# A Mamba layer's scans: the carried state as a column of dt·u·B, dt·u·B issued mid-group, dt·u in four, and weight products beside the scans

## The chip, the cores and the metric

The kernel runs on one core of a Trainium2 chip, all in float32 except for a small part of the graph layer. The metric is the device time of one execution in microseconds, as the median of several runs. TensorE (PE) multiplies matrices, VectorE (DVE), ScalarE (ACT) and GpSimd (POOL) work on tiles of 128 partitions, and SyncE (SP) issues most transfers.

## The reference

The network has four layers on an input of 2 images, 256 channels, 48 x 48 positions (L = 2304 positions in each image). Only layer 0, the start of layer 1 and the start of layer 2 matter here.

Layer 0 is a Mamba layer with a forward and a backward branch. Each branch works on 512 inner channels with 16 states each:

```
xs = silu(causal_conv4(xi) + conv_b)
dt = softplus(proj_dt(xs) @ dtproj.T + dtproj_b)          # one value per channel and position
h[t] = exp(dt[t] * A) * h[t-1] + (dt[t] * u[t]) * B[t]     # u = xs, 16 states per channel
y[t] = sum over states of h[t] * C[t]  +  D * xs[t]
out  = x + ((y_f + y_b) * silu(z)) @ out_proj.T
```

Layer 1 begins with a group norm of each image (32 groups of 8 channels). Layer 2 begins with an attention of three heads. For each head h the kernel multiplies the weights first: the 256 x 256 products of the query's and key's weights, and of the value's and output's weights, are stacked in one array "gm", and the biases give a small array "ub".

## The kernel before

**Tiling.** Layer 0 goes through the positions in pieces of W = 384 (NCH = 6 pieces an image). For each image the forward branch runs over its six pieces, and then the backward branch over the same pieces from the last to the first: 24 pieces in the order (image 0 forward, image 0 backward, image 1 forward, image 1 backward). The 512 channels are DB = 4 blocks of 128 partitions.

**One piece.** `scan` goes through 16 groups. A group is one block d and GN = 4 of the 16 states, and blocks go in pairs (d0, d0+1). For each pair and set of states, SP loads B and C rows broadcast to all partitions (tiles bb and cc, 768 KB each). For each group POOL computes `db` = dtu * B for four states in one instruction (L359). For each state ACT computes `hs` = exp(dt*A) into PSUM (L376), DVE runs the recurrence with tensor_tensor_scan (L382 forward, L385 backward) and multiplies by C (`hc`, L390); for six of sixteen states POOL does that product instead, and then the scan writes to the tile `ho`. PE adds the 16 products of a block into PSUM by a multiplication with the identity (`yp`, L344). The scan starts from the last piece's state:

```
init = 0.0 if step == 0 else state[:, d, n : n + 1]
nc.vector.tensor_tensor_scan(to, hs, db[:, j], init, ALU.mult, ALU.add)
...
nc.scalar.copy(state[:, d, n : n + 1], last)
```

**Beside the scans.** Three generators are advanced between the states, at 32 slots a piece (one after every second state): `prepare` makes the next piece's xs, dt and dtu (15 steps, ended at slot 25), `project_in` makes the inner channels of a later piece (12 steps, over 32 slots, in the first ten pieces only), and `project_out` ends a backward piece. A pair such as `(prepare(...), 15, 25)` says how many steps there are and by which slot they are to be done. The end of `prepare` is the softplus: exponential and +1 on ACT (L302, L305), Ln and -1 on ACT (L307, L308), three 1536-wide operations on DVE (L310 to L312), and the product dtu = dt * xs on POOL in one 1536-wide instruction (L314). While scans run, `prepare`, `project_in` and `project_out` get their PSUM bank from one pool with a single bank, tag "mm".

**Order.** The code is written in this order; a scheduler of the framework then orders the instructions of each engine by priority, which is the order of the program, among those that it holds to be ready, so that small moves happen. Each engine then runs its list in order, and so does SP's queue of transfers.

**Layers 1 and 2.** Layer 1 starts with `group_norm(0)`: statistics of 12 pieces (L517), two small products with the matrix `gmat`, and the scaling into `xn` (L533). The first product of layer 1 that needs it is `pk` (L547). Beside layer 1 the edge lists of the graph layer are sorted on DVE, which `sort_rest` ends. `layer2_attn` then loads the weights of each head (`w_eo`), multiplies them (L713, L721) and copies them to `gm` and `ub`; the transposes of the values (L741) and the query product `pq` (L750, emptied by ACT into `qq`, L754) follow.

Of the kernel before, what the change touches and what calls it, by code (L numbers as in the profile page):

```python
# [27 lines left out]
P = 128  # L28
# [24 lines left out]
class Env:  # L53
# [20 lines left out]

    def uid(self):
        self.n_pools += 1
        return self.n_pools
# [7 lines left out]
def bc(ap, shape, axis):  # L85

    return ap.unsqueeze(axis).to_broadcast(shape)
# [31 lines left out]

def load_x(E, b, c):  # L120
    xin = E.p["x"].rearrange("b (k p) n -> p b k n", p=P)
    E.nc.sync.dma_start(
        E.xres[:, :, b * L + c * W : b * L + (c + 1) * W], xin[:, b, :, c * W : (c + 1) * W]
    )
# [4 lines left out]
def layer0(ctx, E):  # L129

# [32 lines left out]
    def hold():  # L163

        pool, tag = (ps, "mm") if scanning else (psh, "hs")
        return pool.tile([P, W], F32, tag=tag, name="mm")

    def project_in(b, c):
# [15 lines left out]
        rs = up.tile([P, W], F32, tag="rs", name="rs")  # L184
# [53 lines left out]
    one = big.tile([P, 2], F32, name="one")  # L238
    nc.vector.memset(one[:, 0:1], 1.0)
    nc.vector.memset(one[:, 1:2], -1.0)  # L240
# [11 lines left out]
    def prepare(b, s, c, got):  # L252
# [39 lines left out]
        dt = wp.tile([P, DB, W], F32, tag="dt", name="dt")  # L292
# [12 lines left out]
        nc.scalar.activation(dtu, ex, AF.Identity, bias=one[:, 0:1])  # L305
        yield
        nc.scalar.activation(ln, dtu, AF.Ln)  # L307
        nc.scalar.activation(dtu, dtu, AF.Identity, bias=one[:, 1:2])  # L308
        yield
        nc.vector.tensor_tensor(ex, ex, dtu, ALU.subtract)  # L310
        nc.vector.tensor_tensor(dt, dt, ln, ALU.add)
        nc.vector.tensor_tensor(dt, dt, ex, ALU.add)  # L312
        yield
        nc.gpsimd.tensor_tensor(dtu, dt, xs, ALU.mult)  # L314
        got.extend((b, s, c, xs, y, dt, dtu, bcd))
        yield

# [13 lines left out]
    def scan(step, beside, b, s, c, xs, y, dt, dtu, bcd):  # L331

        fwd = s == "f"
        yp = [None] * DB
# [17 lines left out]
        for d0, g in [(d0, g) for d0 in range(0, DB, 2) for g in range(NS // GN)]:  # L352
            bb = wp.tile([P, GN, W], F32, tag="bb", name="bb")
            nc.sync.dma_start(bb, bcd[16 + g * GN : 16 + (g + 1) * GN, :].partition_broadcast(P))
            cc = wp.tile([P, GN, W], F32, tag="cc", name="cc")
            nc.sync.dma_start(cc, bcd[32 + g * GN : 32 + (g + 1) * GN, :].partition_broadcast(P))
            for d in (d0, d0 + 1):
                db = wp.tile([P, GN, W], F32, tag="db", name="db")
                nc.gpsimd.tensor_tensor(db, bc(dtu[:, d, :], [P, GN, W], 1), bb, ALU.mult)  # L359
                if g == 0:  # L360

                    while waiting and waiting[0][1] < d0:
                        add_state(*waiting.pop(0)[1:])
                    yp[d] = psy.tile([P, W], F32, tag=f"y{d % 2}", name=f"yp{d}")
                    nc.tensor.matmul(
                        yp[d], lhsT=w_d[s][:, d, :], rhs=xs[:, d, :], start=True, stop=False
                    )
                    if not fwd:
                        nc.tensor.matmul(
                            yp[d], lhsT=E.ident, rhs=yf[:, d, :], start=False, stop=False  # L370
                        )
                for j in range(GN):
                    n = g * GN + j
                    on_pool = j in GP[(g + d) % 2]
                    hs = psh.tile([P, W], F32, tag="hs", name="hs")
                    nc.scalar.activation(  # L376
                        hs, dt[:, d, :], AF.Exp, scale=nega[s][:, d * NS + n : d * NS + n + 1]
                    )
                    to = wp.tile([P, W], F32, tag="ho", name="ho", bufs=4) if on_pool else hs
                    init = 0.0 if step == 0 else state[:, d, n : n + 1]  # L380
                    if fwd:
                        nc.vector.tensor_tensor_scan(to, hs, db[:, j], init, ALU.mult, ALU.add)  # L382
                        last = to[:, W - 1 : W]
                    else:
                        nc.vector.tensor_tensor_scan(  # L385
                            to[:, ::-1], hs[:, ::-1], db[:, j, ::-1], init, ALU.mult, ALU.add
                        )
                        last = to[:, 0:1]
                    hc = wp.tile([P, W], F32, tag="hcp" if on_pool else "hc", name="hc", bufs=4)
                    (nc.gpsimd if on_pool else nc.vector).tensor_tensor(hc, to, cc[:, j, :], ALU.mult)  # L390
                    if step < NCH - 1:
                        nc.scalar.copy(state[:, d, n : n + 1], last)  # L392
                    while waiting and waiting[0][0] + LAG <= at:
                        add_state(*waiting.pop(0)[1:])
                    if on_pool:
                        waiting.append((at, d, hc))
                    else:
                        add_state(d, hc)
                    at += 1
                    if j % 2:  # L400
                        slot += 1
                        for i, (steps, n_steps, end) in enumerate(beside):
                            while done[i] * end < n_steps * slot and next(steps, beside) is not beside:
                                done[i] += 1
# [4 lines left out]
        for steps, _, _ in beside:  # L409
            for _ in steps:  # L410
                pass

# [7 lines left out]
    for _ in prepare(0, "f", 0, ready):  # L420
        pass
    scanning = True
    pieces = [(0, c) for c in range(2, NCH)] + [(1, c) for c in range(NCH)]
    after = None
    for i, (b, s, step, c) in enumerate(order):
        now, ready = ready, []
        beside = [(after, 2, 5)] if after else []
        if i + 1 < len(order):
            nb, s2, _, c2 = order[i + 1]
            beside.append((prepare(nb, s2, c2, ready), 15, 25))  # L430
        if i < len(pieces):
            beside.append((project_in(*pieces[i]), 12, 32))
        scan(step, beside, *now)
# [26 lines left out]
def layer1(ctx, E, edges):  # L460
# [21 lines left out]
    gmat = big.tile([P, P], F32, name="gmat")  # L482
    same_block(E, lw, gmat, 3, 1.0 / 8)
# [26 lines left out]
    def group_norm(b):  # L510

        xb = E.xres[:, :, b * L : (b + 1) * L]
        mv = wp.tile([P, 2, 2], F32, tag="mv", name="mv")
        for k in range(2):
            st = wp.tile([P, NCH, 6], F32, tag="st", name="st")
            for c in range(NCH):
                nc.vector.bn_stats(st[:, c, :], xb[:, k, c * W : (c + 1) * W])  # L517
            nc.vector.bn_aggr(mv[:, k, :], st)
        pg = ps.tile([P, 2], F32, tag="mm", name="pg")
        nc.tensor.matmul(pg, lhsT=gmat, rhs=mv[:, :, 0], start=True, stop=True)  # L520
        gm = wp.tile([P, 2], F32, tag="gm", name="gm")
        nc.vector.tensor_copy(gm, pg)
        dv = wp.tile([P, 2], F32, tag="dv", name="dv")
        nc.vector.tensor_tensor(dv, mv[:, :, 0], gm, ALU.subtract)
        nc.vector.tensor_tensor(dv, dv, dv, ALU.mult)
        nc.vector.tensor_tensor(dv, dv, mv[:, :, 1], ALU.add)
        gv = ps.tile([P, 2], F32, tag="mm", name="gv")
        nc.tensor.matmul(gv, lhsT=gmat, rhs=dv, start=True, stop=True)
        gr = wp.tile([P, 2], F32, tag="gr", name="gr")
        nc.scalar.activation(gr, gv, AF.Sqrt, bias=E.eps[1e-5])  # L530
        nc.vector.reciprocal(gr, gr)
        for k in range(2):
            nc.vector.tensor_scalar(  # L533
                E.xn[:, k, b * L : (b + 1) * L], xb[:, k, :], gm[:, k : k + 1], gr[:, k : k + 1],
                ALU.subtract, ALU.mult,
            )
# [150 lines left out]
def layer2_attn(ctx, E):  # L687
# [3 lines left out]

    nc, tc, p = E.nc, E.tc, E.p
    NH, D = 3, 768
    S = L // NH
    DT, ST, HW2 = D // P, S // P, S // 2
# [4 lines left out]
    ub = big.tile([P, NH, 4], F32, name="ub")  # L700
    with (
        tc.tile_pool(name="l2wt", bufs=2) as wts,
        tc.tile_pool(name="l2wps", bufs=2, space=PSUM) as ps,
    ):
        for h in range(NH):

            w_eo = wts.tile([P, DT, 2 * C], F32, tag="w_eo", name="w_eo")
            nc.sync.dma_start(w_eo[:, :, 0:C], p["W_embed"][h].rearrange("(k p) m -> p k m", p=P))
            nc.sync.dma_start(w_eo[:, :, C:], p["W_outT"].rearrange("(k p) m -> p k m", p=P))
            for m in range(2):  # L710
                pg = ps.tile([P, 2 * C], F32, tag="pg", name="pg")
                for k in range(DT):
                    nc.tensor.matmul(  # L713
                        pg, lhsT=w_eo[:, k, m * P : (m + 1) * P], rhs=w_eo[:, k, :],
                        start=k == 0, stop=k == DT - 1,
                    )
                nc.vector.tensor_copy(gm[:, h, m, :], pg)
# [1248 lines left out]
```

## Time and profile before

| | us |
|---|---|
| median of 3 runs | 5448.44 (5447.45 to 5450.56) |
| the profiled execution | 5416.49 |
| its span, from the first to the last instruction | 5414.7 |
| first db product (L359) of the scans | 95.9 |
| last output product of layer 0 starts | 2398 |
| first pk of layer 1 (L547) | 2417.2 |
| first pq of layer 2 (L750) | 3181.6 |

A row of the profile names an operation by the engine, the line of the kernel and the tile that it writes and reads ("hs<-hs,state,db"). Times are microseconds unless marked ns. A fence with starts is a timeline: start, duration, engine, line, operation. A fence with "<-" between two operations is a list of waits: who waited, for whom, and then the total in us, how many times, and the longest. The row of busy tenths has 40 slices of 135 us each.

### The profile page before, as it was taken

The page shows a single profiled execution, that of the slowest core. Times are in us where ns is not written, and L with a number is a line of the kernel's source. Part 1 is how long each engine was busy: PE and PEld are TensorE (multiplying, and loading weights), DVE is VectorE, ACT ScalarE, POOL GpSimd, SP SyncE. Part 2 cuts the span into 40 slices and gives each one's busy share as a digit, 9 for nine tenths or more (in the row PEclk, how much of TensorE's full clock was granted, in tenths as well). Part 3 has the DMA queues.
Part 4 walks back from the last instruction along what each step waited for, and adds up shares of the span by engine and source line. Part 5 has one row for each costly group of instructions (what it writes and reads, how often), then busy time and mean ns, then how long its engine had stood idle before and what let it go on. Part 6 is the DMA issues. An engine that isn't in the chain of part 4 may idle for free. (4 is left out here: it accounts for less than half of the span.)

```text
span 5414.7 us, 47212 instructions
## 1 busy us (share of the span) xinstructions
PE 4771.7 (88%) x15246; PEld 2653.7 (49%) x15246; DVE 3503.3 (65%) x5360; ACT 2365.8 (44%) x4935; POOL 2410.2 (45%) x1308
## 2 busy tenths in 40 slices
PE   7888888888877778769999999999999999999897
PEld 3444444443333334335555555556654455555675
DVE  4899898898999898899996234447634401212343
ACT  5767777666667666632222213332123222222111
POOL 3888887788999888860000000008802100000321
PEclk8999999999999889989999989999999999999898
DMA  4445454443545444431110010011122200000422
GB/s 162 163 170 179 161 177 171 156 150 140 172 148 178 152 152 158 146 138 33 40 38 6 0 39 0 27 36 30 22 71 55 61 3 9 6 9 8 84 82 93
DMA packets 178083, 491.28 MB, mean 91 GB/s; under 512 B 32182, under 2 KB 100666, under 8 KB 177562
## 3 DMA queue, kind: packets, MB, share of 16 engines
q1 hardware_dynamic: 169114, 475.36, 25.6%
q0 software_dynamic: 8704, 12.73, 1.6%
q8 instruction: 124, 2.03, 0.2%
q14 instruction: 141, 1.16, 0.1%
HBM read 416.44 MB, written 71.58 MB: 90 GB/s over the span
## 5 line engine op out<-in xcount | busy, mean ns | idle before, releaser
L344 PE MATMUL yp<-hc,ident 128*128 128x384 f32 x3072 | 1203.1, 525 | 291.6 <-DVE hc L390 251.7
L359 POOL TENSOR_TENSOR db<-dtu,bb 128x1536 f32<-128x1536 f32 x384 | 1332.3, 3471 | 49.7 <-issue 19.1
L344 PEld LDWEIGHTS yp<-hc,ident 128*128 128x128 f32 x3072 | 577.1, 199 | 873.5 <-DVE hc L390 447.6
L390 POOL TENSOR_TENSOR hc<-ho,cc 128x384 f32<-128x384 f32 x576 | 579.4, 1014 | 185.3 <-DVE ho L382 83.3
L390 DVE TENSOR_TENSOR hc<-hs,cc 128x384 f32<-128x384 f32 x960 | 498.5, 540 | 39.1 <-PE yp L344 37.8
L376 ACT ACTIVATE hs<-dt,negab 128x384 f32<-128x384 f32 x768 | 434.2, 581 | 93.3 <-DVE ho L385 42.1
L376 ACT ACTIVATE hs<-dt,negaf 128x384 f32<-128x384 f32 x768 | 433.4, 581 | 55.0 <-DVE hc L390 25.5
L385 DVE TENSOR_TENSOR_SCAN hs<-hs,state,db 128x384 f32<-128x384 f32 x400 | 395.1, 1010 | 56.0 <-POOL db L359 30.3
L382 DVE TENSOR_TENSOR_SCAN hs<-hs,state,db 128x384 f32<-128x384 f32 x400 | 396.1, 1010 | 30.2 <-POOL db L359 22.9
L1771 POOL DMA_INDIRECT xe<-xt_d,token x48 | 47.4, 987 | 754.3 <-issue 716.0
L266 PE MATMUL mm<-xw,w_cv 128*128 128x384 f32 x768 | 287.5, 510 | 67.2 <-ACT xs L270 29.4
L1706 PE MATMUL po<-at,xtok 128*128 128x384 f32 x864 | 329.9, 507 | 7.7 <-ACT at L1704 7.5
L912 POOL PARTITION_ALL_REDUCE most<-most x1 | 0.4, 380 | 738.6 <-DVE most L911 738.6
L1697 PE MATMUL sp<-qT,xn 128*128 128x384 f32 x864 | 317.4, 487 | 0.0
L1704 ACT ACTIVATE at<-sp 128x384 f32<-128x384 f32 x216 | 104.6, 490 | 472.7 <-PE sp L1697 472.6
L1354 PE MATMUL ph<-xn,w 128*128 128x384 f32 x768 | 288.2, 519 | 19.3 <-ACT hid L1358 7.6
L627 PE MATMUL pf<-t,wfc 128*128 128x384 f32 x768 | 255.5, 489 | 0.0
L646 PE MATMUL po<-hid,wfc 128*128 128x384 f32 x768 | 253.6, 486 | 0.0
L385 DVE TENSOR_TENSOR_SCAN ho<-hs,state,db 128x384 f32<-128x384 f32 x240 | 240.0, 1000 | 15.2 <-ACT hs L376 15.1
L382 DVE TENSOR_TENSOR_SCAN ho<-hs,state,db 128x384 f32<-128x384 f32 x240 | 239.5, 998 | 8.4 <-ACT hs L376 8.2
L266 PEld LDWEIGHTS mm<-xw,w_cv 128*128 128x128 f32 x768 | 145.9, 196 | 195.1 <-ACT xs L270 46.9
L392 ACT COPY state<-hs 128x1 f32<-128x1 f32 x800 | 117.5, 155 | 278.2 <-DVE hc L390 276.3
(433 smaller groups left out, 7947.6 us busy)
## 6 DMA issues: line engine op xcount, KB each, us to landing
bb<-bcd SPq DMA_DIRECT2D x192, 768.0 KB, 4.1
cc<-bcd SPq DMA_DIRECT2D x192, 768.0 KB, 4.1
xw<-xi_d SPq DMA_DIRECT2D x24, 774.0 KB, 5.3
w<-in_m_w SPq DMA_DIRECT2D x16, 1024.0 KB, 5.8
y_d<-y SPq DMA_DIRECT2D x32, 384.0 KB, 2.3
ye<-y_d SPq DMA_DIRECT2D x32, 384.0 KB, 3.5
xi_d<-xz SPq DMA_DIRECT2D x48, 192.0 KB, 3.0
z_d<-xz SPq DMA_DIRECT2D x48, 192.0 KB, 3.2
```

The source lines that it names most:

```text
L266: nc.tensor.matmul(px, lhsT=w_cv[b, s][:, d * 4 + k, :], rhs=xw[:, d, o : o + W], start=k == 0, stop=k == 3,)
L344: nc.tensor.matmul(yp[d], lhsT=E.ident, rhs=hc, start=False, stop=summed[d] == NS)
L359: nc.gpsimd.tensor_tensor(db, bc(dtu[:, d, :], [P, GN, W], 1), bb, ALU.mult)
L376: nc.scalar.activation(hs, dt[:, d, :], AF.Exp, scale=nega[s][:, d * NS + n : d * NS + n + 1])
L382: nc.vector.tensor_tensor_scan(to, hs, db[:, j], init, ALU.mult, ALU.add)
L385: nc.vector.tensor_tensor_scan(to[:, ::-1], hs[:, ::-1], db[:, j, ::-1], init, ALU.mult, ALU.add)
L390: (nc.gpsimd if on_pool else nc.vector).tensor_tensor(hc, to, cc[:, j, :], ALU.mult)
L627: nc.tensor.matmul(pf, lhsT=wfc1[:, k, f * P : (f + 1) * P], rhs=t1[:, k, :], start=k == 0, stop=k == 1,)
L646: nc.tensor.matmul(po[m], lhsT=wfc2[:, f, m * P : (m + 1) * P], rhs=hid[:, i, :], start=f == 0, stop=f == 15,)
L1354: nc.tensor.matmul(ph, lhsT=w1[:, e, k, f * P : (f + 1) * P], rhs=xn[:, k, c * W : (c + 1) * W], start=k == 0, stop=k == 1,)
L1697: nc.tensor.matmul(sp, lhsT=xn[:, k, t0 + i * P : t0 + (i + 1) * P], rhs=qT[:, k, c * W : (c + 1) * W], start=k == 0, stop=k == 1,)
L1706: nc.tensor.matmul(po[m], lhsT=xtok[:, i, m * P : (m + 1) * P], rhs=at, start=i == 0, stop=i == MT - 1,)
```

## The change

Five things are done:

1. **State as a column.** The tiles hs, ho, db and dt (now `dts`) get one column more, ahead of the piece in the scan's direction. dts is 0 there, so that exp gives 1; db holds the last piece's state there, which POOL copies from `state` (a memset of 0 in a first piece). The scan starts from the immediate 0.0, over 385 columns, and its first result is the carried state.
2. **db mid-group.** `begin_group` issues the loads of bb and cc and the db of the next group (at a piece's end the next piece's first) after the second state of the current one.
3. **Softplus and dtu.** L308 goes; its -1 is done in a scalar_tensor_tensor on DVE. The three DVE operations have a step each, with an empty step after Ln, and dtu is four 384-wide instructions in four steps. `prepare` has 21 steps now, to be done by slot 29.
4. **Weight products.** `head_products` computes gm and ub in twelve parts beside pieces 10 to 21, one part of three steps a piece, and stores gm to DRAM (`gm_d`). Layer 2 loads it back.
5. **Group statistics.** `group_stats` of image 0 run beside the second forward piece of image 1; layer 1 only scales. `gmat` is built at the start of the kernel. In layer 3 one normalization takes its buffers from a pool of its own with single buffers.

The core of the diff:

```diff
-    def scan(step, beside, b, s, c, xs, y, dt, dtu, bcd):
+    def begin_group(q, first_piece, b, s, c, xs, y, dts, dtu, bcd):
+        d0, g, d = groups[q]
+        if d == d0:
+            for n, o in (("bb", 16), ("cc", 32)):
+                held[n] = wp.tile([P, GN, W], F32, tag=n, name=n)
+                nc.sync.dma_start(held[n], bcd[o + g * GN : o + (g + 1) * GN, :].partition_broadcast(P))
+        lead, body = (0, slice(1, W + 1)) if s == "f" else (W, slice(0, W))
+        db = wp.tile([P, GN, W + 1], F32, tag="db", name="db")
+        nc.gpsimd.tensor_tensor(db[:, :, body], bc(dtu[:, d, :], [P, GN, W], 1), held["bb"], ALU.mult)
+        if first_piece:
+            nc.gpsimd.memset(db[:, :, lead : lead + 1], 0.0)
+        else:
+            nc.gpsimd.tensor_copy(db[:, :, lead], state[:, d, g * GN : (g + 1) * GN])
+        return db, held["cc"]
...
-                    hs = psh.tile([P, W], F32, tag="hs", name="hs")
+                hs = psh.tile([P, 512], F32, tag="hs", name="hs")[:, : W + 1]
...
-                        nc.vector.tensor_tensor_scan(to, hs, db[:, j], init, ALU.mult, ALU.add)
+                nc.vector.tensor_tensor_scan(
+                    to[:, way], hs[:, way], db[:, j, way], 0.0, ALU.mult, ALU.add
+                )
...
+                if j == 1:
+                    if q + 1 < len(groups):
+                        begun = begin_group(q + 1, step == 0, b, s, c, xs, y, dts, dtu, bcd)
+                    elif following:
+                        begun = begin_group(0, step == NCH - 1, *following)
```

In `prepare`:

```diff
+        dts = wp.tile([P, DB, W + 1], F32, tag="dt", name="dt")
+        nc.vector.memset(dts[:, :, lead : lead + 1], 0.0)
+        dt = dts[:, :, body]
...
         nc.scalar.activation(ln, dtu, AF.Ln)
-        nc.scalar.activation(dtu, dtu, AF.Identity, bias=one[:, 1:2])
         yield
-        nc.vector.tensor_tensor(ex, ex, dtu, ALU.subtract)
+        yield
+        nc.vector.scalar_tensor_tensor(ex, dtu, -1.0, ex, ALU.add, ALU.subtract)
+        yield
         nc.vector.tensor_tensor(dt, dt, ln, ALU.add)
-        nc.vector.tensor_tensor(dt, dt, ex, ALU.add)
         yield
-        nc.gpsimd.tensor_tensor(dtu, dt, xs, ALU.mult)
+        nc.vector.tensor_tensor(dt, dt, ex, ALU.subtract)
+        yield
+        for d in range(DB):
+            nc.gpsimd.tensor_tensor(dtu[:, d, :], dt[:, d, :], xs[:, d, :], ALU.mult)
+            yield
...
-            beside.append((prepare(nb, s2, c2, ready), 15, 25))
+            beside.append((prepare(nb, s2, c2, ready), 21, 29))
...
+        elif i < len(pieces) + 12:
+            beside.append((islice(heads, 3), 3, 32))
+        if (b, s, step) == (1, "f", 1):
+            beside.append((group_stats(E, up, lambda: hold()[:, 0:2], 0), 15, 32))
```

The weight products, one part for each head h, half m and half z of the inner dimension:

```diff
+                t = up.tile([P, 2, W], F32, tag=("pos", "h", "sq")[k], name="w_eo")
+                t = t.rearrange("p k w -> p (k w)")[:, : 2 * C]
+                nc.sync.dma_start(t[:, 0:C], p["W_embed"][h, rows, :])
+                nc.sync.dma_start(t[:, C:], p["W_outT"][rows, :])
...
+            pg = ps.tile([P, 2 * C], F32, tag="mm", name="pg")
+            for k in range(3):
+                nc.tensor.matmul(pg, lhsT=w_eo[k][:, m * P : (m + 1) * P], rhs=w_eo[k], start=k == 0, stop=k == 2)
+            if z == 0:
+                nc.scalar.copy(part, pg)
+            else:
+                nc.vector.tensor_tensor(part, part, pg, ALU.add)
+                nc.sync.dma_start(E.gm_d[h, m], part)
+            yield
+            pu = ps.tile([P, 2 * C], F32, tag="mm", name="pu")
...
```

In layer 2 the loop over the heads with its loads and products goes, and this takes its place:

```diff
+    for h in range(NH):
+        nc.sync.dma_start(gm[:, h], E.gm_d[h].rearrange("m p c -> p m c"))
```

`group_stats(E, wp, bank, b)` holds the statistics part of the old `group_norm` unchanged, with a yield after each bn_stats and each small step, 15 steps in all.

## The prediction

> **What bounds the kernel now.** I read the page's busy table and slices first, then equal-length windows over single scan pieces, then the waits of VectorE and GpSimd inside the scan stage, then the timeline at the places which the diff touches.
>
> ```profile
> PE 4771.7 (88%) x15246; PEld 2653.7 (49%) x15246; DVE 3503.3 (65%) x5360; ACT 2365.8 (44%) x4935; POOL 2410.2 (45%) x1308
> DVE  4899898898999898899996234447634401212343
> POOL 3888887788999888860000000008802100000321
> ```
>
> The shares of the whole span mislead: VectorE (DVE) is at 65%, but in slices 2 to 17, the 96 to 2392 us of the scans, it is at 8 or 9 tenths with GpSimd (POOL) close behind. Afterwards TensorE (PE) is at 9 and POOL is idle. So the diff touches two regimes. The starts of the dtu product (L314) lie one piece apart; windows between them cut out a forward piece of batch 1, a forward and a backward piece of batch 0 (both with a projection beside them) and a backward piece of batch 1:
>
> ```profile
> 1527.20:1616.60 89.40, 71.53 (x193) 33.55 (x192) 86.67 (x108) 61.94 (x155) 82.56 (x41) 0.98 0.45 159
> 358.60:455.10 96.50, 79.59 (x225) 39.55 (x224) 89.51 (x114) 69.46 (x168) 83.14 (x43) 1.00 0.49 169
> 854.30:958.60 104.30, 87.99 (x250) 44.89 (x249) 91.32 (x119) 72.31 (x166) 81.30 (x42) 0.98 0.46 163
> 2094.20:2190.40 96.20, 75.39 (x208) 38.37 (x208) 85.41 (x114) 64.70 (x153) 81.29 (x41) 0.96 0.44 156
> ```
>
> The columns are PE, weight loads, DVE, ACT, POOL. DVE idles 2.7, 7.0, 13.0 and 10.8 us of a piece: the plain forward piece is DVE-bound, the others lose time to waits. Over the stage these are the largest:
>
> ```profile
> DVE hs L382 <- POOL db L359: 39.1, 34, 6.8
> DVE hc L390 <- PE yp L344: 37.8, 33, 9.7
> DVE hs L385 <- POOL db L359: 35.3, 34, 2.5
> DVE dt L311 <- ACT state L392: 24.4, 12, 3.6
> DVE ho L385 <- ACT hs L376: 18.7, 14, 2.9
> ```
>
> They come at one place of each piece, about 70% through, where Ln, its table loads, three wide DVE steps (L310 to L312) and the wide dtu product follow each other. Outside the scans one line matters: between layers 1 and 2, ACT's first qq waits 58.7 us for PE, which multiplies weights by weights.
>
> ```profile
> ACT qq L754 <- PE pq L750: 96.6, 23, 58.7
> ```
>
> **The scan's initial value: -74 us of DVE.** With an operand, two scans hold DVE for 1.83 us until the next start (0.915 each); with the immediate 0.0 of a first piece, for 1.71 (0.855 each):
>
> ```profile
> 359.95 1.02 DVE L382 TENSOR_TENSOR_SCAN hs<-hs,state,db 128x384 f32<-128x384 f32 x1
> 360.87 1.00 DVE L382 TENSOR_TENSOR_SCAN ho<-hs,state,db 128x384 f32<-128x384 f32 x1
> 361.78 0.54 DVE L390 TENSOR_TENSOR hc<-hs,cc 128x384 f32<-128x384 f32 x1
> ...
> 120.85 0.95 DVE L382 TENSOR_TENSOR_SCAN hs<-hs,db 128x384 f32<-128x384 f32 x1
> 121.72 0.93 DVE L382 TENSOR_TENSOR_SCAN ho<-hs,db 128x384 f32<-128x384 f32 x1
> 122.56 0.53 DVE L390 TENSOR_TENSOR hc<-hs,cc 128x384 f32<-128x384 f32 x1
> ```
>
> The page has 400+240+400+240 = 1280 scans with an operand: 1280 x 0.06 = 77 us. The 385th column costs about 0.855/384 = 2 ns on all 1536, 3 us. That is 3.7 us less DVE work in each of 20 pieces. The memset of dts' zero column (four elements, some 0.07 us like the memsets at the start) counts nothing on DVE: 24 x 0.07 = 2 us at worst.
>
> **The state column: POOL gets 384 small copies or memsets.** None is in the trace. From below I take 0.10 us (POOL's 128x1 memsets). From the two POOL products, 1014 ns for 384 elements and 3439 for 1536, the slope is 2.1 ns and the intercept 0.21 us; I take that, with 0.10 and the 1.0 us of a whole 384-wide product as ends. 16 x 0.21 = 3.4 us a piece. Behind each copy in POOL's queue stand that group's products hc, and the scans wait for the copy. Its source was written by ACT one piece earlier, so it waits for nothing itself.
>
> **Softplus and dtu.** ACT loses L308, 24 x 1.57 = 38 us, and the DVE steps move one scheduling slot (3 us) apart, with an empty slot after Ln. The DVE waits of L311 (24.4 on ACT's state copy, 7.5 on Ln) and L310 (4.4 and 1.3) should end: -38. The waits of the scans for ACT's exponentials, 18.7+13.1+11.2+9.3+10.7 = 63, fall by half, because the table loads remain: -31. The dtu product is 3.43 us in one block; in four (4 x 0.955) other POOL work passes between, and with db issued mid-group I take half of the 74 us of waits for db away: -37. The new slots 21 of 29 end dtu by slot 29; db of the next piece starts at 31, so 2 slots of cover remain; without it a piece boundary would show up to 4 us of waiting.
>
> Against this speaks a lock, and here row and rule differ:
>
> ```profile
> 1609.91 4.95 POOL L359 TENSOR_TENSOR db<-dtu,bb 128x1536 f32<-128x1536 f32 x1
> 1611.96 4.51 DVE L312 TENSOR_TENSOR dt<-dt,ex 128x1536 f32<-128x1536 f32 x1
> ```
>
> Alone these take 3.44 and 1.74; overlapping, both stretch. Yet the median of L312 is 1.742, and all three steps together average (44.0+45.0+53.6)/23 = 6.2 us a piece against 3 x 1.74 = 5.2, since today POOL mostly stands idle in that burst. The rows alone would add nothing for the new order. The Trainium skill, "SBUF — State Buffer", "Who interferes with whom", says that a DVE instruction with two SBUF inputs and a GpSimd instruction that reads SBUF exclude each other for the whole instruction. If so, spreading the steps into a busy POOL makes each collide: the mean rest of a POOL instruction is (16 x 3.4² + 28 x 0.955²)/(2 x 81) = 1.3 us, so 3 x 1.3 = 3.9 a piece instead of 1.0: +67 us over 23 pieces for DVE, and POOL is held 3 x 1.74 = 5.2 us a piece. I take the rule, since the plain forward piece (L310 3.06, L311 1.91, L312 4.51 in one piece) already behaves so. The row would give 60 us more gain.
>
> **The scan stage summed by kind of piece.** POOL after: 16 x 3.39 + 28 x 0.955 = 81, +3.4 copies, +5.2 held = 89.5. DVE busy after: the four windows less 3.7, plus 2.9 of lock where it isn't paid today: 83.0, 88.7, 90.5, 84.6. Idle left, about half: 2.7, 2.5, 7, 6.
> - Six forward pieces of batch 1: DVE 86, POOL 89.5, as today: 0.
> - Forward, batch 0: 91.2 instead of 96.5; 5 x 5.3 and 3 for the first piece: -29.
> - Backward, batch 0: 97.5 instead of 104.3 in four of them, about 5 in the other two, which are shorter: -37.
> - Backward, batch 1: 90.6 instead of 96.2; 5 x 5.6, and 2 for the last piece, which prepares nothing: -30.
> - The prelude (dtu in four before the first db): -3.
> Sum -99, of 2296 us.
>
> **Weight products moved beside the scans.** Twelve pieces get 6 matmul records of 0.593 and 12 of about 0.2 each: 6 us of PE, which idles 18 to 21 us of these pieces; on top ACT or DVE empties a bank (0.6 or 0.7 us). They share the one "mm" bank with prepare and project_out, so PE can stand behind an emptying, and a late yp makes hc late (the 37.8 us above). Six loads of 128 KB a piece go through SP ahead of bb and cc, 6 x 0.4 = 2.4 us of issue, at 45% DMA use; the products come ten slots later, so they don't wait. I charge 0.7 us a piece, +8; ends 0 and 12 x 6 = 72.
>
> **Group statistics of batch 0.** 12 bn_stats at 0.46 and small steps, 7 us of DVE in one piece: +7. At layer 1's start this clears the path from 2399.2 to the first pk at 2417.2. Left there: the xn scaling (2.85 us, which I expect behind the 4.27 us memset of img on POOL) and wqkv's load, issued at 2398.85, some 5 us. First pk near 2406: -11, ends 0 and -15.
>
> **Layer 2's start.** PE's last layer-1 matmul ends near 3112; the first pq comes at 3181.6:
>
> ```profile
> 3118.11 5.19 PEld L721 LDWEIGHTS pu<-vec,w_eo 128*128 128x128 f32 x24 [3.14 <-issue]
> 3181.60 0.88 PE L750 MATMUL pq<-xn,gm 128*128 128x384 f32 x1
> ```
>
> After: three loads of gm (512 KB; w_eo's halves of 768 KB landed in 5.0 to 11.0), and the transposes, whose copies queue on DVE behind some 10 us of sort_rest. First pq at about 3127: -54, ends -40 and -62. The attention is PE-bound after that, so the lead stays. The matrix of the group norm is now built at the start, where DVE idles until 7.8 us and POOL until 92 (uncovered: some 1.5 us). The normalization with single buffers in layer 3 runs beside PE-bound attention (uncovered: a few us of its DVE steps once). Both 0.
>
> **Sum.** -99 +8 +7 -11 -54 = -149 on the profiled execution, 5416.5 us (span 5414.7 and 1.8 around it). The timed median is 5448.4, 0.6% more; the difference carries over as it is: about 5299.
>
> **Rivals.**
> 1. POOL becomes the bound everywhere: copies of 0.4 us, each of the steps blocking a db. Then POOL's 81 + 6.4 + 5.2 = 93, with 2 to 3 of hand-over, is today's mean piece (95.6), and the 99 us fall to nothing: -50, 5398. For it: POOL is already over 80 busy in every window. Against: it still idles 7 to 23 us there.
> 2. The lock is avoided as in today's median, and the waits end wholly: 67 + 30 us more, 5202. For it: emptying the burst is what the spread does. Against: POOL's own floor.
> 3. Slower: the small POOL copy costs far more than its elements. Pieces equal today's mean plus what layers 1 and 2 save, (95.6 + 50/24) = 97.7, when (97.7 - 0.5 - 86.1)/16 = 0.69 us a copy. At 1.0 us a piece is 86.1 + 16 + 0.5 = 102.6, +168 in the scans and -50 elsewhere: 5566. Against: even POOL's 128x128 iota takes 0.24.
> 4. Layer 2 does not start earlier, because its transposes and gm loads still queue (behind sort_rest until 3143): -20 instead of -54, 5333.
>
> **How the numbers follow.** Main case and its variant 4: 0.68, with 5255 to 5360 from the ends of its terms. Rival 1: 0.17. Rival 2: 0.09. Rival 3: 0.06. A measurement of this kernel can tell about 0.2%, 11 us, from no change. Faster 0.92, same 0.02 (rival 1 with a bad start of layer 2), slower 0.06. The range 5235 to 5405 holds the main case and most of rival 1, and leaves out rivals 2 and 3 and the far ends.
>
> **What would show it.** Right: scans 0.855 apart in all pieces; POOL copies near 0.2; L311's and L310's waits gone, these steps over 2.5 us on average; forward pieces of batch 1 at about 89, backward ones near 91 and 98; first pq 10 to 18 us after layer 1's last matmul. Wrong: POOL copies above 0.5; DVE waiting more for db than 74 us; pieces of 12 longer by PE's full 6 us; or qq still waiting 40 us or more.

## The result, and the profile after

The changed kernel takes 5440.71 us (median of 20 runs, 5430.69 to 5449.36); the kernel before, beside it on the same chip, takes 5456.51 (5447.26 to 5463.13). The ratio is 0.9972 [0.9965, 0.9978]: faster by 15 us, where 149 were forecast. The profiled execution of the changed kernel has a span of 5429.9 us.

The first traces of before and after can't be set side by side over the whole span: the products fp of layer 3, which no edit touches, last 191 us in the trace of before and 230 in that of after. As the last section shows, this goes with the chip. So both kernels were profiled once more on one chip (pair_before, pair_after). There fp lasts 229 us in both. The rows give shortest, median and longest duration in ns, then the first and the last start:

```profile
L1086 PE MATMUL fp<-wide,ol x256: 466/466/531, 3760.5 to 3989.6; 128*128 128x360 f32 x128
```

```profile
L1160 PE MATMUL fp<-wide,ol x256: 466/466/531, 3756.8 to 3985.0; 128*128 128x360 f32 x128
```

On that chip the spans, 5442.4 and 5435.0, divide like this:

| us | before | after | difference | forecast |
|---|---|---|---|---|
| start to layer 0's last output product | 2395.2 | 2451.9 | +56.7 | -84 |
| from there to the first pk | 19.0 | 6.6 | -12.4 | -11 |
| layer 1's products, pk to the last po | 691.9 | 692.6 | +0.7 | 0 |
| last po to the first pq of layer 2 | 67.4 | 14.0 | -53.4 | -54 |
| the rest | 2268.9 | 2269.9 | +1.0 | 0 |

The forecast of the first row is its -99 for the scans with +8 and +7 for the work laid beside them. Everything outside the scan stage came as written. In the first two traces the stage lost 46 us; either way the error is some 130 to 140 us, all of it in the scans. The whole scan stage of pair_before and of pair_after (the columns are the stretch and its length, then the busy time of PE, weight loads, DVE, ACT and POOL, the granted clock of PE, and the DMA's busy share and GB/s):

```profile
96.00:2395.00 2299.00, 1859.51 (x5011) 918.78 (x5012) 2083.63 (x2692) 1553.52 (x3577) 1966.52 (x986) 0.95 0.45 160
```

```profile
94.00:2452.00 2358.00, 1936.01 (x5244) 980.10 (x5242) 2067.29 (x2761) 1533.07 (x3563) 2046.91 (x1437) 0.94 0.46 160
```

DVE is busy for 16 us less (2067.3 for 2083.6), but it idles for 290.7 us instead of 215.4. The granted clock hardly differs, and a product yp lasts 526 ns on average, where it lasted 524: PE is not slower at the products that DVE waits for.

The page of the changed kernel, busy times and the tenths of DVE and POOL:

```profile
PE 4782.7 (88%) x15246; PEld 2664.3 (49%) x15246; DVE 3467.9 (64%) x5395; ACT 2340.8 (43%) x4914; POOL 2490.2 (46%) x1764
...
DVE  4988888888888888899997244546544501212343
...
POOL 3888887888898898890000000038502200000331
```

In slices 3 to 17 DVE has gone from eights and nines to eights, and POOL stands at 8, with a few sevens and nines, as before. Over the span DVE has 35 us less to do (3467.9 for 3503.3) and POOL 80 more (2490.2 for 2410.2). (POOL's digits from slice 24 on are work of later layers, with PE at 9.) The windows over one piece of each kind, between starts of the dtu product, in the order of the prediction:

```profile
1543.40:1635.40 92.00, 75.99 (x209) 38.36 (x208) 80.88 (x111) 60.39 (x156) 84.89 (x61) 0.94 0.47 167
349.10:447.40 98.30, 81.62 (x225) 41.56 (x224) 86.19 (x114) 68.92 (x168) 84.72 (x60) 0.97 0.48 165
857.60:961.90 104.30, 89.49 (x249) 46.96 (x248) 89.78 (x120) 70.85 (x166) 86.49 (x61) 0.95 0.47 164
2130.10:2228.50 98.40, 80.69 (x229) 41.06 (x228) 86.33 (x119) 64.12 (x153) 87.80 (x61) 0.97 0.47 165
```

DVE's work fell in the first three (80.9 for 86.7, 86.2 for 89.5, 89.8 for 91.3), about as forecast, and POOL's rose by 1.6 to 6.5; in the fourth DVE has 0.9 us more to do, with five more instructions. The pieces did not get shorter: 92.0, 98.3, 104.3 and 98.4 us, where they were 89.4, 96.5, 104.3 and 96.2. What DVE no longer does, it waits. Its waits in the scan stage (total us, times, longest):

```profile
DVE hs L488 <- POOL db L439: 98.7, 66, 3.5
DVE hc L492 <- PE yp L457: 69.4, 45, 8.5
DVE hs L488 <- ACT hs L483: 31.0, 34, 2.4
DVE hs L488 <- POOL db L437: 19.9, 13, 3.3
DVE ho L488 <- ACT hs L483: 19.4, 21, 2.1
DVE ex L352 <- ACT dtu L346: 15.0, 10, 2.3
DVE hs L488 <- POOL db L433: 14.8, 5, 4.3
```

The waits for ACT are shorter. Those for db, 74 us before, are 98.7 + 19.9 + 14.8 = 133, most of them now ended by the small copy L439 (L437 is the memset of first pieces); those for yp are 69.4 instead of 37.8. At the start of layer 2, ACT's longest wait for a query product is 7.5 us, where it was 58.7:

```profile
ACT qq L828 <- PE pq L824: 10.6, 4, 7.5
```

### The profile page after: what moved, and what is told of

Same layout as the page of the kernel before. It is cut to its first block, busy times and chain, and to the rows that moved or that the text cites. A ratio compares the mean times of both kernels' runs of the same rounds, so it can differ in the third digit from the quotient of the medians.

```text
span 5429.9 us, 48029 instructions
## 1 busy us (share of the span) xinstructions
PE 4782.7 (88%) x15246; PEld 2664.3 (49%) x15246; DVE 3467.9 (64%) x5395; ACT 2340.8 (43%) x4914; POOL 2490.2 (46%) x1764
## 5 line engine op out<-in xcount | busy, mean ns | idle before, releaser
L488 DVE TENSOR_TENSOR_SCAN hs<-hs,db 128x385 f32<-128x385 f32 x960 | 893.5, 951 | 168.0 <-POOL db L439 98.7
L492 POOL TENSOR_TENSOR hc<-ho,cc 128x384 f32<-128x384 f32 x576 | 600.2, 1048 | 213.0 <-DVE ho L488 140.3
L488 DVE TENSOR_TENSOR_SCAN ho<-hs,db 128x385 f32<-128x385 f32 x576 | 540.1, 938 | 19.5 <-ACT hs L483 19.4
L492 DVE TENSOR_TENSOR hc<-hs,cc 128x384 f32<-128x384 f32 x960 | 498.1, 538 | 71.6 <-PE yp L457 69.4
L483 ACT ACTIVATE hs<-dt,negab 128x385 f32<-128x385 f32 x768 | 438.0, 582 | 87.3 <-DVE hc L492 44.1
L483 ACT ACTIVATE hs<-dt,negaf 128x385 f32<-128x385 f32 x768 | 435.4, 582 | 66.8 <-DVE hc L492 30.7
L304 PE MATMUL mm<-xw,w_cv 128*128 128x384 f32 x768 | 302.6, 534 | 69.5 <-DVE xres L373 32.7
L1432 ACT ACTIVATE hid<-ph,vec 128x384 f32<-128x384 f32 x192 | 110.6, 581 | 332.3 <-PE ph L1428 241.2
L1781 PEld LDWEIGHTS po<-at,xtok 128*128 128x128 f32 x864 | 149.8, 189 | 177.2 <-ACT at L1779 108.4
```

Of the source, the lines that this page charges most:

```text
L304: nc.tensor.matmul(px, lhsT=w_cv[b, s][:, d * 4 + k, :], rhs=xw[:, d, o : o + W], start=k == 0, stop=k == 3,)
L483: nc.scalar.activation(hs, dts[:, d, :], AF.Exp, scale=nega[s][:, d * NS + n : d * NS + n + 1])
L488: nc.vector.tensor_tensor_scan(to[:, way], hs[:, way], db[:, j, way], 0.0, ALU.mult, ALU.add)
L492: (nc.gpsimd if on_pool else nc.vector).tensor_tensor(hc, to[:, body], cc[:, j, :], ALU.mult)
L1781: nc.tensor.matmul(po[m], lhsT=xtok[:, i, m * P : (m + 1) * P], rhs=at, start=i == 0, stop=i == MT - 1,)
```

## The experiments

The theory after the result: once POOL carries copies, dtu and db for pieces of 90 to 100 us at 85 us of its own work, the pieces are set by POOL's list and the handing over between POOL and DVE, so that taking time off DVE is worth nothing, and POOL's additions cost. The rivals: the weight products hold PE and with it yp; the spread softplus collides with POOL; db mid-group makes a worse order. The letters in the expectations stand for the theory written beside them there.

Lengths of the pieces, between the starts of their first db, in one trace each (24 pieces; the last is left out). The last column is the ratio of the timed medians to the kernel before on the same chip:

| us | six forward, image 0 | six backward, image 0 | six forward, image 1 | five backward, image 1 | ratio |
|---|---|---|---|---|---|
| pair_before | 572.4 | 604.4 | 540.0 | 488.6 | |
| pair_after | 586.8 | 613.6 | 576.0 | 490.2 | 0.9977 |
| no_heads | 586.7 | 614.1 | 553.6 | 481.4 | 1.0027 |
| operand | 572.3 | 617.2 | 561.4 | 489.3 | 0.9930 |
| column_alone | 582.8 | 604.6 | 552.1 | 480.8 | 1.0021 |
| softplus_alone | 572.0 | 603.8 | 547.0 | 485.8 | 1.0000 |
| act_col | 573.2 | 599.9 | 562.3 | 489.8 | 0.9892 |
| less_pool | 558.8 | 593.4 | 554.9 | 475.1 | 0.9829 |
| less_pool_act_col | 557.8 | 587.4 | 561.7 | 474.6 | 0.9801 |

**The kernels themselves again** (before_again, after_again, and the pair).

> The kernel before, profiled a second time. In the first profile the time from layer 2's first pq to layer 3's first pq is 1147 us, in the changed kernel's 1187, although nothing between them was edited, while the timed runs of before are 30 to 45 us above its profiled execution. If that difference belongs to the execution, this profile lies near 5450 us with about 1187 there and a scan stage that ends within 1 us of the first one (2392). If the change causes it (another layout in memory), this profile repeats 1147 and 5416.

> The changed kernel a second time, so that it and the three kernels beside it share a chip. In its first profile the graph layer's part from the first to the last fp product lasts 230 us; it was 188 to 195 in five other profiles. If that belongs to the execution or the chip and not to the kernel, it is near 190 here, the ratio stays near 0.997, and the scan stage again ends 45 to 50 us later than in before.

> The kernel before, unchanged, profiled on the same chip as the next one, so that the two traces can be set side by side. If the chip doesn't matter to the scan stage: layer 0's last output product within 5 us of 2398, the first pk 19 us after it, layer 2's first pq 65 to 70 us after layer 1's last product; the stretch of the fp products in layer 3 near 190 or near 230 us, as the chip has it.

> The changed kernel, unchanged, on the same chip as the run before. If the chip doesn't matter to the scan stage: layer 0's last output product 40 to 50 us later than in the kernel before, the two starts 12 and 56 us shorter, the fp stretch as long as in the kernel before on this chip, and so a ratio of 0.995 to 0.998. If the chip of the first profile lengthened the scan stage: less than 35 us later here, and a ratio below 0.995.

before_again took 5417.14 us in its one run, with 195 us for fp, and after_again again 229 us where 190 were expected. The pair was run for that reason. after_again has a ratio of 0.9972 [0.9964, 0.998], pair_after 0.9977 [0.9969, 0.9985] on another chip. pair_before's last output product starts at 2395.2, and that of pair_after 56.7 us later: the loss in the scan stage is the kernel's, not the chip's.

**Without the weight products beside the scans** (no_heads): layer 2 makes gm and ub itself, as before.

```diff
-        elif i < len(pieces) + 12:
-            beside.append((islice(heads, 3), 3, 32))
```

> The changed kernel with the weight products back at layer 2's start and nothing of them beside the scans. Theory H (the products make TensorE late in the scans: hc waits for yp 69 us instead of 38): pieces 12 to 17 fall from 95.6 to about 90.5, the scan stage gets 30 to 40 us shorter, layer 2 loses its 56: about +20 us against the changed kernel, 1.001 against before. Theory P (GpSimd is the bound, the products are hidden): the scan stage keeps its 2344 us, all of the 56 us is lost: about 1.007 against before.

1.0027 [1.0017, 1.0036], between the values of the two theories. The scan stage ends at 2422.2 instead of 2442.9 (after_again), so the products cost some 21 us there, where theory H gave 30 to 40. Against pair_after the table has 31: 22 in the forward pieces of image 1 and 9 in the backward ones, which hold ten of the twelve parts. (The forward pieces of image 0, which hold none, take 579.9 us in after_again and 586.8 in pair_after; this is the difference between the two figures, and a measure of what a single trace can tell.) As layer 2 then starts late again, the kernel as a whole loses 0.0055 x 5406 = 30 us by it: the products beside the scans pay, at a higher price than charged.

**The state as an operand again** (operand): no column, no copy on POOL.

```diff
-            nc.gpsimd.tensor_copy(db[:, :, lead], state[:, d, g * GN : (g + 1) * GN])
...
-                    to[:, way], hs[:, way], db[:, j, way], 0.0, ALU.mult, ALU.add
+                    to[:, way], hs[:, way], db[:, j, way], init, ALU.mult, ALU.add
```

> The changed kernel with the state as the scan's operand again: no 385th column, no small copies on GpSimd; all else as changed. Theory P (GpSimd is the bound; 384 copies and memsets hold it for 102 us): the scan stage gets 60 to 100 us shorter although every scan takes 0.06 us longer, 0.980 to 0.986 against before. Theory D (VectorE is the bound, the copies are in GpSimd's gaps): it gets 40 to 75 us longer, 1.005 to 1.011.

0.9930 [0.9916, 0.9943], 23 us faster than with the column (0.0042 x 5406). DVE has 71 us more to do over the span (3538.5 for 3467.9), and the waits for db are 73.1 us, as before the change. The forward pieces of image 0 are as long as before, 7 to 15 us shorter than in the traces of the change. The sign is theory P's, the size is not: P gave 0.980 to 0.986. DVE's time is not worth nothing; it is worth less here than POOL's.

**The softplus of before** (old_softplus): -1 on ACT, one block on DVE, dtu in one instruction.

> The changed kernel with softplus and dtu as before: L308 on ScalarE, three VectorE operations in one step, dtu in one instruction, 15 steps by slot 25. Theory L (spread steps collide with GpSimd: scalar_tensor_tensor at 2.8 us on average, small copies stretched to 1.75): 20 to 40 us shorter than the changed kernel, 0.990 to 0.9935. Theory S (the spread does what it says and hides the burst): 40 to 60 us longer, 1.004 to 1.008.

1.0001 [0.9992, 1.0009], the value of neither theory: in the whole change the new softplus is worth 0.0029 x 5456 = 16 us.

**db at the group's start** (group_start).

```diff
-            db, cc = begun
+            db, cc = begin_group(q, step == 0, b, s, c, xs, y, dts, dtu, bcd)
```

> The changed kernel with each group's loads, db and column issued at the start of that group, as before, and no longer after the second state of the group ahead. Theory M (mid-group issue costs: an hc gets between db and its column copy, or db comes later than the scheduler's own order would have it): 20 to 35 us shorter than the changed kernel, about 0.992. Theory N (the scheduler's order was as good, mid-group changes little): within 8 us of it. If mid-group does what it is for, it is 10 to 30 us longer, 0.999 to 1.003.

0.9973 [0.9962, 0.9985], no difference, as theory N had it: POOL's instructions of the scan stage come in the same order, by operation and tile, in this trace and in pair_after's, so where the code issues db is not what orders POOL's list. This rival is out.

**Single parts in the kernel before**: the weight products and statistics (parts_outside), the column (column_alone), the softplus with dtu in four (softplus_alone).

> The kernel before with only the weight products beside the scans and the early group statistics; state operand, softplus, dtu and db as before. Layer 2 gives 56 us and layer 1 some 12, as in both profiles of the changed kernel. If the products cost what taking them out gave (22 us) and the statistics 7, the sum is -39 us, 0.993. If they lie in TensorE's idle time, -65, 0.988. If they disturb the old order more than the new one, above 0.995.

> The kernel before with only the state column: 385 wide scans from 0.0, copies and memsets on GpSimd, db at the group's start. If it costs here what undoing it in the changed kernel gave, +17 to +20 us, 1.0035. Theory P (GpSimd's copies weigh more than VectorE's 74 us): 1.000 to 1.006. By the prediction (VectorE -74, copies in GpSimd's idle time): 0.987.

> The kernel before with only the softplus and dtu edits (no L308, steps spread, dtu in four, 21 steps by slot 29). If it is worth here what undoing it in the changed kernel cost, -24 us, 0.9956. Theory L (the spread steps meet a busy GpSimd and each waits for the lock; before, GpSimd stood idle in the burst): +10 to +40 us, 1.002 to 1.007, most of it in the plain forward pieces. By the prediction's own terms (-106 of waits, +67 of lock): -39, 0.993.

parts_outside 0.9932 [0.9919, 0.9944], column_alone 1.0021 [1.0014, 1.0028], softplus_alone 1.0000 [0.9992, 1.0008]: -37, +11 and 0 us. The first is what was expected, the second is in theory P's range, and the third met none of its three values. Their sum is -26, and all together gave -15. old_softplus, which holds the first two parts without the third (and db mid-group, which made no difference), gave 0 instead of -26: the column and the work beside the scans hinder each other, and the new softplus wins 16 us of that back, though alone it is worth nothing. In column_alone, whose scans take 0.06 us less like those of the whole change, these are the waits for POOL, which were 39.1 and 35.3 before:

```profile
DVE hs L485 <- POOL db L436: 91.3, 71, 4.5
DVE hs L485 <- POOL db L434: 23.6, 16, 4.5
DVE hs L485 <- POOL db L430: 6.6, 1, 6.6
```

**The copies on ACT instead of POOL** (act_col).

```diff
-            nc.gpsimd.memset(db[:, :, lead : lead + 1], 0.0)
+            nc.vector.memset(db[:, :, lead : lead + 1], 0.0)
...
-            nc.gpsimd.tensor_copy(db[:, :, lead], state[:, d, g * GN : (g + 1) * GN])
+            nc.scalar.copy(db[:, :, lead], state[:, d, g * GN : (g + 1) * GN])
```

> The changed kernel, but ScalarE instead of GpSimd copies the state to the column of db (VectorE clears it in first pieces). Theory P (it is GpSimd's time that counts): the 102 us of copies leave GpSimd, the scan keeps its cheaper immediate: 20 to 60 us shorter, 0.986 to 0.993. Theory Q (what counts is that scans wait for one more small instruction in a queue that runs in order): no shorter, or longer, since ScalarE then stands at a db buffer that is not free yet.

0.9892 [0.9878, 0.9907], 44 us faster than the change (0.0080 x 5456), for 102 us of instructions taken off POOL (its busy time falls by 73, to 2417.5), and in theory P's range. DVE's waits for db fall from 133 to 90.4 us.

**16 instead of 24 products hc a piece on POOL**, in the changed kernel (less_pool) and in the one before (before_less_pool).

```diff
-    GP = ((1, 3), (2,))
+    GP = ((1,), (2,))
```

> The changed kernel with 16 instead of 24 of a piece's 64 products by C on GpSimd, and 48 instead of 40 on VectorE: -7.6 us for GpSimd and +3.7 for VectorE a piece. Theory P (GpSimd is the bound now): 24 x 4 to 5, some 100 us shorter less what VectorE then lacks, 0.980 to 0.988. Theory D (VectorE is the bound): up to 24 x 3.7 = 88 us longer, 1.005 to 1.013. Theory B (neither: the loss lies in the bursts of softplus and in waits for TensorE): within 25 us of the changed kernel.

> The kernel before with 16 instead of 24 of a piece's products by C on GpSimd (VectorE +3.7, GpSimd -7.6 us a piece). The same edit took 75 us off the changed kernel. If GpSimd held up the kernel before as well, 40 to 75 us shorter, 0.986 to 0.993. If VectorE was its bound, as the plain forward pieces (86.7 of 89.4 us busy) say, and it is the change that moved the bound: 40 to 88 us longer, 1.007 to 1.016.

0.9829 [0.9814, 0.9845] and 1.0029 [1.0018, 1.0040]. The same edit makes the kernel before 16 us slower (40 to 88 were expected if DVE was its bound) and the changed one 78 us faster (0.0143 x 5456), in theory P's range. The waits of less_pool show where the gain comes from:

```profile
DVE hc L492 <- PE yp L457: 44.9, 38, 3.3
DVE hs L488 <- ACT hs L483: 19.0, 25, 2.8
...
DVE hs L488 <- POOL db L439: 10.5, 16, 0.8
```

98.7 us of waiting for the copy have become 10.5, and 69.4 of waiting for yp 44.9, while DVE has 81 us more to do over the span (3548.9 for 3467.9). In the kernel before, the waits for db fall as well, from 74 to 11 us (these are the lines of before_less_pool), but there DVE's added 92 us (3595.6 for 3503.3) weigh more:

```profile
DVE hs L382 <- POOL db L359: 10.1, 6, 6.8
DVE hs L385 <- POOL db L359: 1.0, 1, 1.0
```

So both engines counted in both kernels. What the change moved is which of them weighs more.

**With POOL relieved, the parts again**: operand instead of column, the column by ACT, 8 products with the column by ACT (`GP = ((1,), ())`), and the old softplus.

> The changed kernel with 16 instead of 24 hc products a piece on GpSimd, and the state as the scan's operand again (no column, no copies on GpSimd). The same with the column measured 0.9829 of the kernel before. Theory P (GpSimd bounded the changed kernel, with 16 products VectorE does): now the 0.06 us per scan (74 us of VectorE) is on the path, so giving the operand back costs some 30 to 74 us: ratio 0.988 to 0.996. Theory Q (GpSimd still bounds with 16 products, the copies still count): a further gain of 10 to 30 us, ratio 0.977 to 0.981.

> 16 products on GpSimd, and the state column written by ScalarE instead of GpSimd. Theory P: GpSimd no longer bounds, so taking its copies away is worth little: 0.980 to 0.984. Theory Q: the copies still count, the 44 us that the same move was worth with 24 products come again at least by half: 0.975 to 0.979. A third outcome, ScalarE's copies now delay the exponentials that VectorE waits for: above 0.984.

> 8 products on GpSimd instead of 16, column by ScalarE. Each moved product costs VectorE 0.49 us, 8 x 0.49 = 3.9 us a piece. Theory P (VectorE already bounds with 16): 22 x 3.9 = 86 us slower than with 16, ratio near 0.996. Theory Q: GpSimd bound with 16, so no slower, 0.98 or below.

> 16 products on GpSimd, column by GpSimd, but softplus and dtu as in the kernel before (-1 on ScalarE, the VectorE steps in one block, dtu in one instruction). With 24 products, undoing this made the changed kernel 16 us slower by its ratios (0.9972 to 1.0001). Theory P (what spread softplus avoided was queueing on a full GpSimd): with GpSimd relieved it is worth less than 10 us, ratio 0.981 to 0.985. Theory S (it removes waits of VectorE for ScalarE whatever GpSimd does, which now count in full as VectorE is the bound): 15 to 38 us slower, 0.986 to 0.990.

- less_pool_operand 0.9880 [0.9864, 0.9896]. The column, which cost 23 us with 24 products on POOL, gains 0.0051 x 5412 = 28 with 16. That is the lower end of what theory P gave.
- less_pool_act_col 0.9801 [0.9788, 0.9815]: just inside P's range, 15 us better than less_pool, at the edge of what the intervals separate. It is the best version here, 5305.40 against 5411.87 us, 108 us faster than the kernel before by its ratio.
- eight_act_col 0.9925 [0.9913, 0.9937], 67 us slower than with 16, where P gave 86: taking still more off POOL no longer pays.
- less_pool_old_softplus 0.9857 [0.9841, 0.9874]: the new softplus is worth 15 us here too, between the two expectations, and the intervals overlap a little. It is worth about the same at both loads of POOL; why it is worth something only beside the other parts stays open.

One forward piece of image 0 (between the starts of first db products) tells the same in one column. In order: the changed kernel, less_pool, less_pool_operand, eight_act_col.

```profile
381.19:479.53 98.34, 81.65 (x225) 41.55 (x224) 86.23 (x114) 68.88 (x167) 84.75 (x61) 0.97 0.48 166
```

```profile
373.21:467.52 94.31, 79.92 (x226) 39.05 (x224) 88.79 (x122) 68.77 (x167) 77.31 (x54) 1.00 0.50 172
```

```profile
373.73:469.10 95.37, 83.61 (x226) 40.95 (x224) 92.56 (x121) 69.35 (x167) 76.33 (x37) 0.95 0.50 170
```

```profile
375.34:470.16 94.82, 80.04 (x224) 38.91 (x224) 92.31 (x130) 71.93 (x184) 67.67 (x28) 1.00 0.48 173
```

With POOL at 84.8 us DVE idles 98.3 - 86.2 = 12.1 us of the piece; with POOL at 77.3 it idles 5.5, at 76.3 2.8, at 67.7 2.5. In the kernel before it was 7.0, with DVE at 89.5 and POOL at 83.1. In these five pieces DVE's idle time is no fixed part: it is the longer, the nearer POOL's load is to DVE's (1.5 us below it in the changed kernel, 6.4 in the kernel before, then 11.5, 16.2 and 24.6).

## Why the prediction was wrong, step by step

Three of the signs for "right" came: the spacing of the scans, copies near 0.2 us (median), and the first pq 14.0 us after layer 1's last product. So did one of those for "wrong": DVE waits more for db than 74 us. Rival 3 is out, since a copy takes 0.30 us on average and not 0.69 or more, and so is rival 4.

**The scan's initial value, -74 us of DVE: right as a duration, wrong as a gain.** Scans start 0.84 to 0.87 us apart:

```profile
1558.67 0.95 DVE L488 TENSOR_TENSOR_SCAN hs<-hs,db 128x385 f32<-128x385 f32 x1
1559.54 0.93 DVE L488 TENSOR_TENSOR_SCAN ho<-hs,db 128x385 f32<-128x385 f32 x1
1560.38 0.53 DVE L492 TENSOR_TENSOR hc<-hs,cc 128x384 f32<-128x384 f32 x1
```

The time is there, as less_pool_operand showed, but it outweighs what the column costs only once POOL has room.

**The state column.** The estimate of 0.21 us holds for the median (179/194/1788 ns), not for the mean:

```profile
L439 POOL COPY db<-state 128x4 f32<-128x4 f32 x320 | 95.3, 298 | 0.0
```

With 7.1 us of memsets that is 102 us of POOL where 3.4 a piece, 81 in all, were written. The larger omission is the place. The prediction saw products hc queued behind the copy; it did not see them get in front of it:

```profile
1584.06 3.42 POOL L433 TENSOR_TENSOR db<-dtu,bb 128x1536 f32<-128x1536 f32 x1
...
1587.44 0.98 POOL L492 TENSOR_TENSOR hc<-ho,cc 128x384 f32<-128x384 f32 x1
...
1588.38 0.18 POOL L439 COPY db<-state 128x4 f32<-128x4 f32 x1
1588.53 0.98 POOL L492 TENSOR_TENSOR hc<-ho,cc 128x384 f32<-128x384 f32 x1
1588.60 1.82 DVE L488 TENSOR_TENSOR_SCAN hs<-hs,db 128x385 f32<-128x385 f32 x2 [1.34 <-POOL db L439]
```

db is ready at 1587.5, but the group's first scan waits for its column until 1588.6, behind a product of the group before. POOL runs here without a gap. In 111 of the 384 groups of this trace one or two products stand between db and its column; in less_pool it is 13.

**Softplus and dtu.** Of the terms -38 (L311 and L310) and -31 (hs) -15 and -13 came: 22.4 us are left of 37.6, and some 50 of 63. The term -37 (waits for db halved) was wrong in sign: 74 became 133. The lock was priced too high for DVE, so that price did not cause the miss:

```profile
L352 DVE SCALAR_TENSOR_TENSOR ex<-dtu,ex 128x1536 f32<-128x1536 f32 x23 | 64.5, 2803 | 16.7 <-ACT dtu L346 15.0 <-ACT state L496 1.4
...
L356 DVE TENSOR_TENSOR dt<-dt,ex 128x1536 f32<-128x1536 f32 x23 | 50.7, 2205 | 0.0
...
L354 DVE TENSOR_TENSOR dt<-dt,ln 128x1536 f32<-128x1536 f32 x23 | 44.6, 1940 | 6.3 <-ACT ln L348 3.3 <-ACT state L496 2.7
```

64.5 + 50.7 + 44.6 = 160 us where it was 143 before: +17, between the row's 0 and the rule's 67. The exclusion itself is there:

```profile
1553.70 3.43 POOL L433 TENSOR_TENSOR db<-dtu,bb 128x1536 f32<-128x1536 f32 x1
...
1556.08 2.67 DVE L356 TENSOR_TENSOR dt<-dt,ex 128x1536 f32<-128x1536 f32 x1
...
1557.08 1.72 POOL L439 COPY db<-state 128x4 f32<-128x4 f32 x1
```

L356 ends 1.6 us after db has ended at 1557.1, so it ran only then, and the copy of four elements ends with L356 at 1558.8. This agrees with the exclusion that the Trainium skill states ("SBUF — State Buffer", "Who interferes with whom"). The copy, 0.18 us long elsewhere, takes 1.72 us here. At this place no scan waited for it, since DVE itself was busy with L356.

**The scan stage summed by kind of piece: the step that failed.** The failed term is "Idle left, about half", with POOL's 89.5 us held as a floor that does not bind. Summed over six pieces of each kind, that term lets DVE's idle time fall from 201 to 109 us; in the pair it rose from 215 to 291, while DVE's busy time fell by 16. By the pair, the pieces changed by: forward image 0 +14 (forecast -29), backward image 0 +9 (-37), forward image 1 +36 (0, and most of the +15 for the work beside), five backward pieces of image 1 +2 (-28). POOL's busy time stayed below the 89.5, at 84.7 to 87.8 in the windows, and still the pieces are 7 to 18 us longer than it. Two engines that take each other's results in fixed orders, each busy for 83 to 92% of the piece, idle in turn here; the length of a piece is then neither engine's busy time. That POOL's load makes DVE idle is shown by less_pool and act_col, which change only that load and its receiver. How much of the idle time comes from the load and how much from the place of the column in POOL's list was not separated. Rival 1 (POOL becomes the bound) named the engine, but with the same kind of sum: the change lies 43 us above its 5398.

**Weight products, +8.** 21 to 31 us, within the ends given (0 to 72). The forward pieces of image 1 pay most, which were DVE-bound with 2.7 us idle. DVE's waits for yp are 69.4 us with them and 61.4 without, so most of their cost comes in other ways, which were not separated. Before the change these waits were 37.8, and with the products and statistics alone 56.4 (parts_outside). In the changed kernel they fall to 47.2 in operand and to 44.9 in less_pool, but stay at 73.8 in act_col. So no single part makes them, and how they come about stays open.

**Group statistics, layer 1's start and layer 2's start.** -12.4 for -11 and -53.4 for -54: right. The waits, loads and queues that were named there are those of the trace.

## What to carry to other kernels

When two engines hand work to each other and both are busy for most of a stage (here 83 to 92%), moving work from one to the other is to be judged on the receiver too. The giver's saving alone says little, since the receiver's added load can make the giver idle. The same edit, the column, gained 28 us or cost 23 here by how the rest was divided. So it pays to try the division again (here one tuple, `GP`) after such an edit; that was worth five times the change. And a tiny instruction that a whole group waits for is better put on an engine with room: here that was ACT, for 44 us with a full POOL and some 15 with a relieved one.

## What the runs showed of the hardware

Chips differ in one stretch and not in another. With the same median of 466 ns for a matmul, fp takes 228 to 232 us on two chips, in all kernels profiled there, and 188 to 196 us on two others; the kernel before has medians of 5453 and 5456 us where fp is slow, and 5406 to 5412 where it is fast. What makes the stretch longer there stays open. So times are compared here only as ratios to the kernel before on the same chip, and traces of different chips only up to the stages that agree.
